# A state-space scan kernel: one three-bank feed tile with a single VectorE multiply, and work of the joins moved between engines

## The chip, the cores and the metric

One core of a Trainium2 chip runs the whole kernel. The metric is the device time of one execution in microseconds (us). The engines are named as in the profile: PE (TensorE), DVE (VectorE), ACT (ScalarE), POOL (GpSimd) and SP (SyncE, which only issues DMAs here).

## The reference

Eight images of 64 x 64 x 96 go through two layers. Nearly all the work is the selective scan of the first: for each image four directions, 192 channels and 16 states, over 4096 positions.

```python
xc = silu(conv3x3_depthwise(x @ in_proj_w.T [first half]) + conv_b)
xs = stack([s0, s1, s0[..., ::-1], s1[..., ::-1]])      # diagonal, antidiagonal, both reversed
dts, Bs, Cs = split(xs @ x_proj_weight)
delta = softplus(dts @ dt_projs_weight + dt_projs_bias)
def step(hst, inp):
    u_t, d_t, B_t, C_t = inp
    hst = hst * exp(d_t[..., None] * A) + (d_t * u_t)[..., None] * B_t[:, :, None, :]
    return (hst, einsum('bkdn,bkn->bkd', hst, C_t))
y = ys + Dk * xs, summed over the four directions, back in image order
yn = (y - mean) * rsqrt(var + 1e-5) * ln_w + ln_b
out = yn * silu(z) @ out_proj_w.T
```

Then come a residual sum, attention without softmax, and a feed-forward layer with fp8 products.

## The kernel before

**Steps and iterations.** `run` cuts each image into 16 steps: `q` = 0 walks the positions forward in 8 chunks of 512, `q` = 1 backward. Two directions and 64 channels fill the 128 partitions, so the 192 channels are G = 3 groups. A step has 16 iterations, one for each state `n`; 2048 iterations in all form the main loop (L1169 to L1206). An iteration works on tiles of 128 x 3 x 512.

**One iteration.** ACT makes the decay, exp(delta A), by three activations, two iterations ahead (L985, three buffers). The feed, (delta u) times a row of B, is made in PSUM in one of three ways, which FEED (L48) names for each state:
- "A" (10 of 16): ACT scales the transposed product `duT` by B into `feedT`, eight activations (L1007), two iterations ahead; PE transposes it back into the feed (`turn`, L1015), four transposes for each group.
- "G" (1 of 16): the same with POOL's multiplies (L998).
- "D" (5 of 16: states 0, 2, 4, 8, 10): PE copies the row of B to all partitions of feed 0 by a product with `pick` (L1017), and DVE multiplies it by `du`, three instructions, the last of them in place (L1032).

DVE then runs three recurrences (`scan`, L1028), one for each group, `h = decay * h + feed`. POOL keeps the last column (L1042) and multiplies h by the row of C, `cc` (L1047), an iteration later. Four iterations behind, PE transposes h into `y`, three banks that gather the 16 states (`reduce`, L1061). After a step's last state `place` copies `y` to SBUF by ACT and stores it: for q = 0 into `part` (L1090), for q = 1 into the two images `wide` (L1104). For q = 1 the stored part is loaded at state 0 (L1056), into the tile of `place`, and added to `y` by three products with the identity (L1074).

**PSUM.** Its eight banks are `y` (three), two work banks, and three tiles `feed0` to `feed2` of one bank each (L896). Before the main loop, and after it, the feed tiles serve as work banks too; after it, so does a tile `y_end` of three banks, cut into three.

**The order on each engine** is the program's. `tc.manual_schedule()` leaves it as written, and waits between engines are derived from which instructions touch which tile. L1192 to L1197 write PE's order within an iteration: the feed transposes of one group for the next iteration, four y transposes, background work, and the same for the next group. DVE's background work stands between scan 1 and scan 2 (L1035).

**Background work** (convolution of the next image, `front`; normalisation, projection, attention and feed-forward of the last one, `tail`) is written as generators that yield an engine and an estimate in us before each piece. `Work.at` lets pieces go at fixed places of an iteration, within a credit for each engine (L274), and LAGS (L239) says how many iterations a piece stands behind the one that it needs.

**prologue** makes what a step needs, two steps ahead: B and C rows, delta by softplus, `du` by POOL (L947, two buffers), its transpose `duT` with three ACT copies (L955).

**join**, in `tail`, takes 512 positions: it sums the two images y by products with the identity (L665), which ACT copies out (L672) while DVE takes statistics from PSUM (L675); normalises by ACT (L681); transposes (L687); multiplies by the gate on DVE (L689); projects with weights into which ln_w and ln_b were folded (L701, L704); copies out (L708) and takes statistics again (L713). `layers` does the same at L809 and L813. The last image's tail runs after the main loop, with eight jobs at once and no scans beside it.

Of the kernel before, what the change touches and what calls it, by code (L numbers as in the profile page):

```python
# [9 lines left out]
F32 = mybir.dt.float32  # L10
# [7 lines left out]
P = 128  # L18
# [48 lines left out]
def weights(tc, const, dram, w):  # L67
# [28 lines left out]
    k.skip = tile("skip", [P, G, P])  # L96
    k.w_ln = tile("w_ln", [HC, 2, DM])
    k.b_ln = tile("b_ln", [HC, 2, DM])
    k.w1q = tile("w1q", [DM, HID], F8)
# [92 lines left out]
    def layers():  # L192
# [7 lines left out]
        yield SPIN  # L200
        with tc.tile_pool(name="prep", bufs=1, side="right") as prep:
            w_out = load("w_out", [HC, 2, DM], w["w_out"], pool=prep)
            ln_w = load("ln_w", [HC, 2], w["ln_w"], pool=prep)
            ln_b = load("ln_b", [HC, 2], w["ln_b"], pool=prep)
            for _ in range(2):
                yield SPIN

            for a in range(2):
                nc.vector.tensor_scalar(k.w_ln[:, a, :], w_out[:, a, :], ln_w[:, a : a + 1], None, ALU.mult)
                nc.vector.tensor_scalar(k.b_ln[:, a, :], w_out[:, a, :], ln_b[:, a : a + 1], None, ALU.mult)  # L210
        with tc.tile_pool(name="prep", bufs=1, side="right") as prep:
# [404 lines left out]
def tail(tc, work, x, out, k, at, b, last=False):  # L616
# [4 lines left out]
    with tc.tile_pool(name=f"t1_{b}", bufs=1, **area) as p1:  # L621
# [5 lines left out]
        with tc.tile_pool(name=f"t2_{b}", bufs=8 if last else 2, **area) as p2:  # L627
# [3 lines left out]
            def join(c):  # L631
# [22 lines left out]
                if last:  # L654
                    yield dve(2.5)
                    nc.vector.tensor_tensor(yn, ys[0], ys[1], ALU.add)
                    for i in range(4):
                        nc.vector.bn_stats(st[:, i, :], yn[:, i, :])
                        nc.vector.bn_aggr(mv[:, i, :], st[:, i, :])
                for j in range(0 if last else 2):  # L660
                    ps = yield bank(0.65)
                    v = view(ps, P, 2, DI)
                    for i in range(2):
                        for d in range(2):
                            nc.tensor.matmul(  # L665
                                v[:, i, :], k.ident, ys[d][:, 2 * j + i, :],
                                start=(d == 0), stop=(d == 1), skip_group_check=True,
                            )
                        if i == 0:
                            yield pe(0.65)  # L670
                    yield act(0.5)
                    nc.scalar.copy(yn[:, 2 * j : 2 * j + 2, :], v)  # L672
                    yield dve(1.0, 0)
                    for i in range(2):
                        nc.vector.bn_stats(st[:, 2 * j + i, :], v[:, i, :])  # L675
                        nc.vector.bn_aggr(mv[:, 2 * j + i, :], st[:, 2 * j + i, :])
                    work.release(ps)
                r, m = yield from rsqrt(nc, p2, k, mv, P, 4, "n")
# [4 lines left out]
                for a in range(2):  # L683
                    ps = yield bank(0.45)
                    v = view(ps, HC, CH)
                    for i in range(4):
                        nc.tensor.transpose(v[:, i * P : (i + 1) * P], yn[:, i, a * HC : (a + 1) * HC], k.ident)  # L687
                    yield dve(0.7)
                    nc.vector.tensor_tensor(yg[:, a, :], v, gate[:, a, :], ALU.mult)  # L689
                    work.release(ps)  # L690
                ps = yield bank(0.65)
                po = view(ps, P, 4, DM)
# [3 lines left out]
                for i in range(4):  # L696
                    if i % 2 == 0:
                        yield pe(1.2)
                    tok = slice(i * P, (i + 1) * P)
                    for a in range(2):  # L700
                        nc.tensor.matmul(  # L701
                            po[:, i, :], yg[:, a, tok], k.w_ln[:, a, :], start=False, stop=False, skip_group_check=True
                        )
                        nc.tensor.matmul(  # L704
                            po[:, i, :], gate[:, a, tok], k.b_ln[:, a, :], start=False, stop=(a == 1), skip_group_check=True
                        )
                yield act(0.5)
                nc.scalar.copy(t, po)  # L708
                if not last:
                    nc.sync.dma_start(out=at.mid[:, s, :], in_=t)  # L710
                yield dve(1.7, 0)
                for i in range(4):
                    nc.vector.bn_stats(st[:, i, :], po[:, i, :])  # L713
                    nc.vector.bn_aggr(mv[:, i, :], st[:, i, :])
                work.release(ps)
                r, m = yield from rsqrt(nc, p2, k, mv, P, 4, "a")
# [66 lines left out]
        with tc.tile_pool(name=f"t3_{b}", bufs=8 if last else 3, **area) as p2:  # L783

            def layers(c):
# [24 lines left out]
                st, mv = tile("st", [P, 4, 6]), tile("mv", [P, 4, 2])  # L810
                yield dve(1.7, 0)
                for i in range(4):
                    nc.vector.bn_stats(st[:, i, :], po[:, i, :])  # L813
                    nc.vector.bn_aggr(mv[:, i, :], st[:, i, :])
                work.release(ps)
                r, m = yield from rsqrt(nc, p2, k, mv, P, 4, "f")
# [43 lines left out]
def run(tc, psum, dram, x, out, w, NB):  # L860
# [34 lines left out]
    made, decays, feeds, hs, carry, sums, other = {}, {}, {}, {}, {}, {}, {}  # L895
    feed = [psum.tile([P, T], F32, tag=f"feed{g}", name=f"feed{g}") for g in range(G)]  # L896
    banks = [psum.tile([P, T], F32, tag=f"bank{i}", name=f"bank{i}") for i in range(2)]
    work = Work(banks + feed)

    def prologue(m):  # L900
# [44 lines left out]
        yield gp(3.4)  # L945
        du = o.du = tile("du", [P, G, T])
        nc.gpsimd.tensor_tensor(du, delta, u, ALU.mult)  # L947
# [11 lines left out]
    def bring(m):  # L959

        b, q, c = steps[m]
        work.finish(lambda: c in image(b).walked)
        u = pool.tile([P, G, T], F32, tag="u", name=f"u_{m}", bufs=2)
        made[m] = SimpleNamespace(u=u, c={})
        for d in range(2):
            nc.sync.dma_start(
                out=u[d * GC : (d + 1) * GC],
                in_=image(b).seq[d][:, c * T : (c + 1) * T].rearrange("(g i) t -> i g t", i=GC),
            )
# [49 lines left out]
    def recur(i):  # L1019
        m, n = divmod(i, NS)  # L1020
        _, q, _ = steps[m]
        h = hs[i] = pool.tile([P, G, T], F32, tag="h", name=f"h_{i}", bufs=6)
        a = decays.pop(i)
        back = slice(None, None, -1) if q else slice(None)

        def scan(g):
            init = carry[m - 1][:, n, g : g + 1] if m % NST else 0.0
            nc.vector.tensor_tensor_scan(h[:, g, back], a[:, g, back], feed[g][:, back], init, ALU.mult, ALU.add)  # L1028

        if FEED[n] == "D":  # L1030
            for g in (1, 2, 0):
                nc.vector.tensor_tensor(feed[g], feed[0], made[m].du[:, g, :], ALU.mult)  # L1032
        scan(0)
        scan(1)
        work.at("V")  # L1035
        scan(2)
# [12 lines left out]
    def reduce(i, part):  # L1049
        m, n = divmod(i, NS)  # L1050
        b, q, c = steps[m]
        if n == 0 and part == 0:
            sums[m] = psum.tile([P, TB * G, P], F32, tag="y", name=f"y_{m}")
            if q:
                other[m] = pool.tile([P, TB * 2 * DI], F32, tag="ys", name=f"y0_{m}")
                nc.sync.dma_start(out=other[m], in_=image(b).part[:, c, :])  # L1056
        y = sums[m]
# [7 lines left out]
        if q and n in (1, 2, 3) and part == 2:  # L1065
            for j in range(4 * (n - 1), 4 * n):
# [4 lines left out]
                )  # L1071
        if q and n in (8, 9, 10) and part == 2:
            j = n - 8
            nc.tensor.matmul(  # L1074
                y[:, 4 * j : 4 * j + 4, :].rearrange("p a c -> p (a c)"), w.ident,
                other[m][:, j * T : (j + 1) * T], start=False, stop=False, skip_group_check=True,
            )
        if part == 2:
            hs.pop(i)

    def place(m):
# [5 lines left out]
        ys = pool.tile([P, TB * 2 * DI], F32, tag="ys", name=f"ys_{m}")  # L1087
        if q == 0:
            nc.scalar.copy(ys, y.rearrange("p j c -> p (j c)"))
            nc.sync.dma_start(out=image(b).part[:, c, :], in_=ys)  # L1090
            return
        rows = ys.rearrange("p (d k c) -> p d k c", d=2, k=TB)
        for d in range(2):
            nc.scalar.copy(
                rows[:, d].rearrange("p k (g i) -> p k g i", i=GC),
                y.rearrange("p (k g) (d i) -> p d k g i", g=G, d=2)[:, d],
            )
            stride = (3 * WW + 1) * DI if d == 0 else (3 * WW - 1) * DI
            for v in range(2):
                for again in range(2):  # L1100
                    first = (c * (T // HH) + v + (again + d) * WW) * DI
                    view = image(b).wide[d][first : first + HH * stride].rearrange("(h x) -> h x", x=stride)
                    view = view[:, 0 : TB * 2 * DI].rearrange("h (k x) -> h k x", k=TB)[:, :, 0:DI]
                    nc.sync.dma_start(out=view, in_=rows[v * HH : (v + 1) * HH, d])  # L1104

    def begin(b):
# [62 lines left out]
    for i in range(total + LAG + 1):  # L1169
        m, n = divmod(i, NS)  # L1170
        b, at = divmod(i, PER)
        if i < total:
            if at == LAG + 1 and b:
                work.finish(all_done)
                work.stream(between(b))
# [28 lines left out]
        if i + 4 < total:  # L1204
            fetch(i + 4)
        feeds.pop(i, None)  # L1206

    work.finish(all_done)
# [83 lines left out]
```

## Time and profile before

| what | us |
|---|---|
| median of 3 runs | 11580.11 (11578.98 to 11580.71) |
| the profiled execution | 11584.24 |
| its span | 11582.5 |
| first scan begins | 243.8 |
| last scan ends | 11318.2 |
| granted TensorE clock, mean | 0.913 |

The main loop is 11,074 us of the span, 5.4 us an iteration. A step without background work takes 73 to 76 us, one beside the convolution 84 to 95, one beside joins 95 to 103, one beside the other layers 82 to 92.

In the profile, a group's line gives line, engine, operation, tile written and tiles read, shapes and count; then busy time in us and the mean of one in ns; then idle time just before them with what ended it. A timeline line gives start, duration, engine, line, operation, tiles and count, and in brackets the idle time before with what ended it.

### The profile page before, as it was taken

Reading aid. Unit: us, or ns where it says so; the run is one execution under the profiler, and the core shown is the slowest. Engines: PE = TensorE matmul, PEld = TensorE weight load, DVE = VectorE, ACT = ScalarE, POOL = GpSimd, SP = SyncE. Lnnn points to the kernel's source line nnn. Section 1 sums busy time; section 2 is a strip of 40 time slices with the busy share of each in tenths; the row PEclk is TensorE's granted clock in tenths of the full one; section 3 lists DMA queues with packets and bytes.
Section 4 is the critical chain, followed back from the end, with each engine's and each line's share of the span. In section 5 each row is a group of like instructions: output and inputs, shape, how many; then the busy total and the mean of one; then the engine's idle time right before and its main releaser. Section 6 shows DMA issues by size and latency. Waiting matters only on the chain.

```text
span 11582.5 us, 187413 instructions
## 1 busy us (share of the span) xinstructions
PE 9540.5 (82%) x63189; PEld 7973.6 (69%) x63189; DVE 9483.5 (82%) x10714; ACT 9430.0 (81%) x19571; POOL 8885.1 (77%) x6799
## 2 busy tenths in 40 slices
PE   6898889788888888888888888988889888887885
PEld 5677677676776667766677766767667676676663
DVE  2988888888878888788887888888888878888893
ACT  3888888878888888888888788887888878888883
POOL 1877887778867887777887788777887778878883
PEclk8999899898999989999899998999999889898996
DMA  3335333533335333353334433354333533332332
GB/s 91 105 91 140 100 91 91 144 107 97 98 96 134 108 105 91 106 135 104 97 98 113 125 100 104 92 133 116 100 92 98 131 107 96 100 97 86 99 97 53
DMA packets 1122757, 1207.26 MB, mean 104 GB/s; under 512 B 452789, under 2 KB 730006, under 8 KB 1121798
## 3 DMA queue, kind: packets, MB, share of 16 engines
q1 hardware_dynamic: 1121798, 1195.28, 37.6%
q8 instruction: 503, 8.24, 0.3%
q14 instruction: 456, 3.74, 0.1%
HBM read 874.83 MB, written 319.98 MB: 103 GB/s over the span
## 4 chain that ended last, share of the span: by engine, by line
PE 25%; POOL 21%; ACT 20%; DVE 15%; issue 11%; DMA 5%; SPq 3%; POOLq 0%; DVEq 0%; ACTq 0%
POOL h L1047 15%; DVE h L1028 9%; ACT feedT L1007 8%; PE y L1061 7%; PE feed L1015 6%; ACT decay L985 6%; DVE feed L1032 3%; DMA cc<-crow 3%; POOL du L947 2%; PE bank L550 2%; PE bank L915 2%; SPq L595 2%; POOL feedT L998 2%; PE bank L953 1%; POOL carry L1042 1%
## 5 line engine op out<-in xcount | busy, mean ns | idle before, releaser
L1047 POOL TENSOR_TENSOR h<-h,cc 128x1536 f32<-128x1536 f32 x2048 | 7076.9, 3455 | 368.8 <-DMA cc<-crow 187.1
L1028 DVE TENSOR_TENSOR_SCAN h<-decay,carry,feed 128x512 f32<-128x512 f32 x5376 | 6529.7, 1263 | 987.1 <-PE feed L1015 769.8
L985 ACT ACTIVATE decay<-delta,a_neg 128x512 f32<-128x512 f32 x6144 | 3971.1, 712 | 1156.1 <-DVE h L1028 1153.3
L1015 PE MATMUL feed<-ident,feedT 128*128 128x128 f32 x16896 | 3066.7, 301 | 1605.6 <-DVE h L1028 1070.5
L1061 PE MATMUL y<-ident,h 128*128 128x128 f32 x24576 | 3820.9, 288 | 127.2 <-POOL feedT L998 112.8
L1015 PEld LDWEIGHTS feed<-ident,feedT 128*128 128x128 f32 x16896 | 2178.8, 153 | 2288.1 <-ACT feedT L1007 882.8
L1007 ACT ACTIVATE feedT<-duT,rows 128x192 f32<-128x192 f32 x10240 | 3672.2, 444 | 23.8 <-PE feed L1015 21.2
L1061 PEld LDWEIGHTS y<-ident,h 128*128 128x128 f32 x24576 | 3127.9, 150 | 515.5 <-issue 335.2
L1042 POOL COPY carry<-h 128x3 f32<-128x3 f32 x2048 | 393.0, 192 | 1615.3 <-DVE h L1028 1545.8
L1032 DVE TENSOR_TENSOR feed<-feed,du 128x512 f32<-128x512 f32 x1920 | 1202.4, 687 | 137.2 <-PE feed L1017 134.6
L1028 DVE TENSOR_TENSOR_SCAN h<-decay,feed 128x512 f32<-128x512 f32 x768 | 882.5, 1201 | 127.3 <-PE feed L1015 87.5
L550 PE MATMUL bank<-wf,xp 97*128 97x192 f32 x4266 | 858.7, 332 | 0.0
L550 PEld LDWEIGHTS bank<-wf,xp 97*128 97x128 f32 x4266 | 691.0, 194 | 24.1 <-issue 13.5
L1017 PE MATMUL feed<-x,pick 77*128 77x512 f32 x1280 | 695.7, 626 | 3.4
L947 POOL TENSOR_TENSOR du<-delta,u 128x1536 f32<-128x1536 f32 x128 | 441.0, 3445 | 316.1 <-ACT delta L942 309.4
L915 PE MATMUL bank<-wx,u 128*128 128x77 f32 x3048 | 413.1, 299 | 36.2 <-DMA u<-seq 36.2
L915 PEld LDWEIGHTS bank<-wx,u 128*128 128x128 f32 x3048 | 407.3, 217 | 44.4 <-issue 39.6
L937 PE MATMUL bank<-x,ws 13*128 13x512 f32 x764 | 434.7, 649 | 1.6 <-ACT x L928 1.6
L998 POOL TENSOR_TENSOR feedT<-duT,rows 128x512 f32<-128x512 f32 x384 | 396.0, 1061 | 0.0
L955 ACT COPY duT<-bank 128x512 f32<-128x512 f32 x383 | 220.7, 576 | 176.4 <-PE bank L953 174.3
L939 DVE COPY delta<-bank 128x512 f32<-128x512 f32 x382 | 256.2, 671 | 56.4 <-PE bank L937 53.6
L1017 PEld LDWEIGHTS feed<-x,pick 77*128 77x128 f32 x1280 | 209.7, 197 | 71.7 <-DVE h L1028 39.5
(278 smaller groups left out, 7544.3 us busy)
## 6 DMA issues: line engine op xcount, KB each, us to landing
cc<-crow SPq DMA_DIRECT2D x4096, 128.0 KB
u<-seq SPq DMA_DIRECT2D x256, 384.0 KB
wide<-ys SPq DMA_DIRECT2D x512, 192.0 KB
ut<-image SPq DMA_DIRECT2D x768, 64.0 KB
seq<-us SPq DMA_DIRECT2D x128, 384.0 KB
part<-ys SPq DMA_DIRECT2D x64, 768.0 KB
y<-part SPq DMA_DIRECT2D x64, 768.0 KB
y<-wide SPq DMA_DIRECT2D x256, 192.0 KB
```

What stands on the lines that cost most here:

```text
L550: nc.tensor.matmul(v[:, j, :], flat[:, o : o + P], k.wf[:, i, :], start=(i == 0), stop=(i == 8), skip_group_check=True)
L915: nc.tensor.matmul(v[:, j, :], u[:, g, j * P : (j + 1) * P], w.wx[:, q, g, :], start=(g == 0), stop=(g == G - 1))
L947: nc.gpsimd.tensor_tensor(du, delta, u, ALU.mult)
L985: nc.scalar.activation(decays[i][:, g, :], made[m].delta[:, g, :], AF.Exp, scale=w.a_neg[:, q, g, n : n + 1])
L998: nc.gpsimd.tensor_tensor(f.rearrange("p (j g) (d c) -> p g j d c", g=G, d=d)[:, g], o.duT.rearrange("p (j g) (d c) -> p g j d c", g=G, d= ...
L1007: nc.scalar.activation(f[part], o.duT[part], AF.Copy, scale=o.rows[:, j, XB + d * NS + n : XB + d * NS + n + 1])
L1015: nc.tensor.transpose(feed[g][:, j * P : (j + 1) * P], feeds[i][:, j * G + g, :], w.ident)
L1017: nc.tensor.matmul(feed[0], w.pick[:, FEED[:n].count("D"), :], made[m].x, start=True, stop=True)
L1028: nc.vector.tensor_tensor_scan(h[:, g, back], a[:, g, back], feed[g][:, back], init, ALU.mult, ALU.add)
L1032: nc.vector.tensor_tensor(feed[g], feed[0], made[m].du[:, g, :], ALU.mult)
L1047: nc.gpsimd.tensor_tensor(hs[i], hs[i], c.unsqueeze(1).to_broadcast([P, G, T]), ALU.mult)
L1061: nc.tensor.matmul(y[:, j, :], hs[i][:, g, r * P : (r + 1) * P], w.ident, is_transpose=True, start=(n == 0 and j % 4 == 0), stop=(n == NS ...
```

## The change

It has these parts:
- The three feed tiles become one tile of three banks, and DVE's three multiplies become one instruction over it, with the groups in reverse order so that bank 0, which is read, is written last.
- `du` gets one buffer instead of two, and waits in the program's order until the step before has made its last "D" multiply (state 10).
- join sums the two y on POOL and takes statistics from SBUF. The gate's multiply leaves DVE: ACT applies ln_w and ln_b on the way out of PSUM, and POOL multiplies by the gate. The projection is one product for each half. Statistics at L713 and L813 read the copy in SBUF, and the bank is released before them.
- place copies by halves for q = 0 too. For q = 1 the part is loaded at state 8 into a tile of its own and added by POOL (`spread`), which then issues the stores.
- The streams of the next image start two iterations later.

```diff
-    feed = [psum.tile([P, T], F32, tag=f"feed{g}", name=f"feed{g}") for g in range(G)]
+    feeding = psum.tile([P, G, T], F32, tag="feed", name="feed")
+    feed = [feeding[:, g, :] for g in range(G)]
...
         yield gp(3.4)
-        du = o.du = tile("du", [P, G, T])
+        while m and not made[m - 1].multiplied:
+            yield "G", 0.0, -1, False
+        du = o.du = tile("du", [P, G, T], 1)
...
         if FEED[n] == "D":
-            for g in (1, 2, 0):
-                nc.vector.tensor_tensor(feed[g], feed[0], made[m].du[:, g, :], ALU.mult)
+            nc.vector.tensor_tensor(
+                feeding[:, ::-1, :], feed[0].unsqueeze(1).to_broadcast([P, G, T]), made[m].du[:, ::-1, :], ALU.mult
+            )
+        if n == FEED.rindex("D"):
+            made[m].multiplied = True
...
-            if q:
-                other[m] = pool.tile([P, TB * 2 * DI], F32, tag="ys", name=f"y0_{m}")
-                nc.sync.dma_start(out=other[m], in_=image(b).part[:, c, :])
+        if q and n == 8 and part == 0:
+            other[m] = pool.tile([P, TB * 2 * DI], F32, tag="y0", name=f"y0_{m}")
+            nc.sync.dma_start(out=other[m], in_=image(b).part[:, c, :])
...
-        if q and n in (8, 9, 10) and part == 2:
-            j = n - 8
-            nc.tensor.matmul(
-                y[:, 4 * j : 4 * j + 4, :].rearrange("p a c -> p (a c)"), w.ident,
-                other[m][:, j * T : (j + 1) * T], start=False, stop=False, skip_group_check=True,
-            )
...
+    def spread(m, rows):
+        b, q, c = steps[m]
+        for d in range(2):
+            yield gp(1.8, 1)
+            nc.gpsimd.tensor_tensor(
+                rows[:, d], rows[:, d], other[m].rearrange("p (d k c) -> p d k c", d=2, k=TB)[:, d], ALU.add
             )
...
-            if at == LAG + 1 and b:
+            if at == LAG + 3 and b:
+                work.finish(lambda: all_done() and not other)
```

In join, with the same at the statistics of `layers`:

```diff
-                for j in range(0 if last else 2):
-                    ps = yield bank(0.65)
...
-                    yield act(0.5)
-                    nc.scalar.copy(yn[:, 2 * j : 2 * j + 2, :], v)
-                    yield dve(1.0, 0)
...
+                else:
+                    yield gp(1.8)
+                    nc.gpsimd.tensor_tensor(yn, ys[0], ys[1], ALU.add)
+                    yield dve(2.1)
+                for i in range(4):
+                    nc.vector.bn_stats(st[:, i, :], yn[:, i, :])
+                    nc.vector.bn_aggr(mv[:, i, :], st[:, i, :])
...
-                    yield dve(0.7)
-                    nc.vector.tensor_tensor(yg[:, a, :], v, gate[:, a, :], ALU.mult)
+                    yield act(0.7)
+                    nc.scalar.activation(
+                        yg[:, a, :], v, AF.Identity, scale=k.ln_w[:, a : a + 1], bias=k.ln_b[:, a : a + 1]
+                    )
                     work.release(ps)
+                yield gp(2.3)
+                nc.gpsimd.tensor_tensor(yg, yg, gate, ALU.mult)
...
-                            po[:, i, :], yg[:, a, tok], k.w_ln[:, a, :], start=False, stop=False, skip_group_check=True
-                        )
-                        nc.tensor.matmul(
-                            po[:, i, :], gate[:, a, tok], k.b_ln[:, a, :], start=False, stop=(a == 1), skip_group_check=True
+                            po[:, i, :], yg[:, a, tok], k.w_out[:, a, :], start=False, stop=(a == 1), skip_group_check=True
...
-                yield dve(1.7, 0)
+                work.release(ps)
+                yield dve(1.7)
                 for i in range(4):
-                    nc.vector.bn_stats(st[:, i, :], po[:, i, :])
+                    nc.vector.bn_stats(st[:, i, :], t[:, i, :])
```

In `weights`, ln_w and ln_b are loaded as they are, and the two folded weights and their four DVE instructions go.

More of the change, by code (lines that the diff above doesn't have):

```diff
@@ L96, in weights @@
     k.skip = tile("skip", [P, G, P])
-    k.w_ln = tile("w_ln", [HC, 2, DM])
-    k.b_ln = tile("b_ln", [HC, 2, DM])
     k.w1q = tile("w1q", [DM, HID], F8)
@@ L200, in layers @@
         yield SPIN
[L201 to L210, printed above, removed]
+        k.w_out = load("w_out", [HC, 2, DM], w["w_out"])
+        k.ln_w = load("ln_w", [HC, 2], w["ln_w"])
+        k.ln_b = load("ln_b", [HC, 2], w["ln_b"])
+        yield SPIN
         with tc.tile_pool(name="prep", bufs=1, side="right") as prep:
@@ L656, in join @@
                     nc.vector.tensor_tensor(yn, ys[0], ys[1], ALU.add)
-                    for i in range(4):
-                        nc.vector.bn_stats(st[:, i, :], yn[:, i, :])
-                        nc.vector.bn_aggr(mv[:, i, :], st[:, i, :])
-                for j in range(0 if last else 2):
-                    ps = yield bank(0.65)
-                    v = view(ps, P, 2, DI)
-                    for i in range(2):
-                        for d in range(2):
-                            nc.tensor.matmul(
-                                v[:, i, :], k.ident, ys[d][:, 2 * j + i, :],
-                                start=(d == 0), stop=(d == 1), skip_group_check=True,
-                            )
-                        if i == 0:
-                            yield pe(0.65)
-                    yield act(0.5)
-                    nc.scalar.copy(yn[:, 2 * j : 2 * j + 2, :], v)
-                    yield dve(1.0, 0)
[L674 to L677, printed above, removed]
+                else:
[5 more added lines that the diff above has]
+                    nc.vector.bn_aggr(mv[:, i, :], st[:, i, :])
                 r, m = yield from rsqrt(nc, p2, k, mv, P, 4, "n")
@@ L697, in join @@
                     if i % 2 == 0:
-                        yield pe(1.2)
+                        yield pe(0.65)
                     tok = slice(i * P, (i + 1) * P)
@@ L710, in join @@
                     nc.sync.dma_start(out=at.mid[:, s, :], in_=t)
-                yield dve(1.7, 0)
+                work.release(ps)
+                yield dve(1.7)
                 for i in range(4):
-                    nc.vector.bn_stats(st[:, i, :], po[:, i, :])
+                    nc.vector.bn_stats(st[:, i, :], t[:, i, :])
                     nc.vector.bn_aggr(mv[:, i, :], st[:, i, :])
-                work.release(ps)
                 r, m = yield from rsqrt(nc, p2, k, mv, P, 4, "a")
@@ L810, in layers @@
                 st, mv = tile("st", [P, 4, 6]), tile("mv", [P, 4, 2])
-                yield dve(1.7, 0)
+                work.release(ps)
+                yield dve(1.7)
                 for i in range(4):
-                    nc.vector.bn_stats(st[:, i, :], po[:, i, :])
+                    nc.vector.bn_stats(st[:, i, :], t[:, i, :])
                     nc.vector.bn_aggr(mv[:, i, :], st[:, i, :])
-                work.release(ps)
                 r, m = yield from rsqrt(nc, p2, k, mv, P, 4, "f")
@@ L963, in bring @@
         u = pool.tile([P, G, T], F32, tag="u", name=f"u_{m}", bufs=2)
-        made[m] = SimpleNamespace(u=u, c={})
+        made[m] = SimpleNamespace(u=u, c={}, multiplied=False)
         for d in range(2):
@@ L1071, in reduce @@
                 )
-        if q and n in (8, 9, 10) and part == 2:
-            j = n - 8
-            nc.tensor.matmul(
-                y[:, 4 * j : 4 * j + 4, :].rearrange("p a c -> p (a c)"), w.ident,
-                other[m][:, j * T : (j + 1) * T], start=False, stop=False, skip_group_check=True,
-            )
         if part == 2:
@@ L1087, in place @@
         ys = pool.tile([P, TB * 2 * DI], F32, tag="ys", name=f"ys_{m}")
[L1088 to L1091, printed above, removed]
         rows = ys.rearrange("p (d k c) -> p d k c", d=2, k=TB)
@@ L1096, in place @@
                 y.rearrange("p (k g) (d i) -> p d k g i", g=G, d=2)[:, d],
+            )
+        if q == 0:
+            nc.sync.dma_start(out=image(b).part[:, c, :], in_=ys)
+        else:
+            work.start(spread(m, rows), urgent=True)
+    def spread(m, rows):
[4 more added lines that the diff above has]
+                rows[:, d], rows[:, d], other[m].rearrange("p (d k c) -> p d k c", d=2, k=TB)[:, d], ALU.add
             )
@@ L1104, in place @@
                     nc.sync.dma_start(out=view, in_=rows[v * HH : (v + 1) * HH, d])
+        other.pop(m)
     def begin(b):
@@ L1206, in run @@
         feeds.pop(i, None)
+    work.finish(lambda: not work.urgent)
     work.finish(all_done)
```

## The prediction, made before the result was known

> **What bounds the kernel now.** First the table of engines and the chain of work that ended last.
>
> ```profile
> PE 9540.5 (82%) x63189; PEld 7973.6 (69%) x63189; DVE 9483.5 (82%) x10714; ACT 9430.0 (81%) x19571; POOL 8885.1 (77%) x6799
> PE 25%; POOL 21%; ACT 20%; DVE 15%; issue 11%; DMA 5%; SPq 3%; POOLq 0%; DVEq 0%; ACTq 0%
> ```
>
> No engine is full and none owns the chain: the kernel lives on overlap. So the costliest groups are read next, for what the overlap is between.
>
> ```profile
> L1028 DVE TENSOR_TENSOR_SCAN h<-decay,carry,feed 128x512 f32<-128x512 f32 x5376 | 6529.7, 1263 | 987.1 <-PE feed L1015 769.8
> L1015 PE MATMUL feed<-ident,feedT 128*128 128x128 f32 x16896 | 3066.7, 301 | 1605.6 <-DVE h L1028 1070.5
> L1032 DVE TENSOR_TENSOR feed<-feed,du 128x512 f32<-128x512 f32 x1920 | 1202.4, 687 | 137.2 <-PE feed L1017 134.6
> ```
>
> The feed is a ring of two: PE writes it (L1015, L1017), DVE reads it (L1028), and each waits for the other, some 1 us at a time. Only 987 us of DVE's 11,582 go to this, because the three feeds are three tiles: once scan 0 is over, PE refills feed 0 while DVE runs scans 1 and 2. The timeline of PE, then of DVE, shows that:
>
> ```profile
> 3003.84 0.63 PE L1015 MATMUL feed<-ident,feedT 128*128 128x128 f32 x4 [2.12 <-DVE h L1028]
> 3004.86 0.66 PE L1015 MATMUL feed<-ident,feedT 128*128 128x128 f32 x4
> 3005.97 0.66 PE L1015 MATMUL feed<-ident,feedT 128*128 128x128 f32 x4
> ...
> 3002.47 6.78 DVE L1028 TENSOR_TENSOR_SCAN h<-decay,feed 128x512 f32<-128x512 f32 x6
> ```
>
> The three fours start 1.0 to 1.1 us apart, at the pace of the scans, and DVE runs six scans without a pause.
>
> The change makes the three tiles one tile of three banks. What happens then is in this trace, in its last 200 us: there the tile y_end (three banks, used as three work banks) stands beside the tiles feed, with the same instructions.
>
> ```profile
> 11392.46 5.27 PE L687 MATMUL feed<-ident,y 128*96 128x128 f32 x12
> 11394.26 0.69 DVE L689 TENSOR_TENSOR yg<-feed,gate 96x512 f32<-96x512 f32 x1 [1.07 <-PE feed L687]
> 11396.08 0.69 DVE L689 TENSOR_TENSOR yg<-feed,gate 96x512 f32<-96x512 f32 x1 [1.14 <-PE feed L687]
> 11397.72 5.26 PE L687 MATMUL y_end<-ident,y 128*96 128x128 f32 x12
> 11403.02 1.28 DVE L689 TENSOR_TENSOR yg<-y_end,gate 96x512 f32<-96x512 f32 x2 [4.57 <-PE y_end L687]
> ...
> 11424.78 0.48 ACT L708 COPY t<-feed 128x384 f32<-128x384 f32 x1 [3.74 <-PE feed L704]
> 11441.67 1.24 ACT L708 COPY t<-y_end 128x384 f32<-128x384 f32 x3 [12.18 <-PE y_end L704]
> ...
> 11537.67 0.56 ACT L836 CAST h<-y_end 128x512 f16<-128x512 f32 x1
> 11538.28 1.44 PE L834 MATMUL y_end<-xq,w1q 96*128 96x512 fp8e5 x3 [0.99 <-ACT h L836]
> ```
>
> From the tiles feed, a read starts after each four matmuls (1.8 us apart). From y_end the first read starts after all twelve, 4.57 us idle, though its own bank was full after four; ACT's three copies come together after 12.18 us. The other direction too: PE writes y_end again 0.05 us after the third read's end (11537.67 + 0.56), though the first bank's read began at 11535.19. So the program's waits treat a PSUM tile as a whole, whichever bank is touched. This decides the forecast.
>
> **The change part by part. The feed's tile** (L896). With one tile, refill waits for scan 2 instead of scan 0, and scan 0 waits for the last refill instead of the first. The loop then alternates: DVE alone, PE alone. Prices, all from this trace:
> - From a scan's end to PE's start 0.15 us (median of 826); from the last transpose's start to the scan's 0.41 us (739 cases).
> - Between them PE issues, in the order of L1192 to L1197, 12 feed transposes with the first 8 of the y transposes between: 19 steps of 0.11 us, 2.1 us. A gap of **2.65 us** ahead of an iteration fed by transposes, 11 of 16, 1408 in all.
> - Ahead of a "D" iteration only the pick is between: 0.15 us, and 1.06 from its start to the multiply's: **1.21 us**, 640 times.
> - Three scans back to back: 2 x 1.12 + 1.26 = 3.50 us, 2048 times.
> - Other DVE work that L1035 puts between scan 1 and scan 2 now delays PE: 777 us from first to last scan, L689 (which goes) left out. Other PE work lying between the feed transposes: 694 us, without the removed lines.
>
> **The multiply** (L1032). Three take 1.87 us from first start to last end. One of 1536 elements is not in the trace. Rows: 687 ns for 512, 958 for 768 (L656); the slope of 1.06 ns an element gives 958 + 768 x 1.06 = 1.77 us. Bounds 1.60 and 1.88. Taken: 1.77, 640 times, a gain of 64 us.
>
> Sum at full TensorE clock: 1408 x 2.65 = 3731; 640 x 1.21 = 774; 2048 x 3.50 = 7168; 640 x 1.77 = 1133; 777; 694; the stretch ahead of the first scan 244 and behind the last 264. Total **14,785 us**.
>
> **The clock.** PE now pauses in every iteration, some 2.5 to 3.5 us. After pauses with full pace before them, the trace shows half pace (0.21 us a step instead of 0.11) in 16 of 61 cases at 2 to 2.5 us, 14 of 26 at 2.5 to 3, and 65 of 101 at 3 to 3.5. One such case, which lasts 3.3 us:
>
> ```profile
> 3012.54 1.08 PE L1015 MATMUL feed<-ident,feedT 128*128 128x128 f32 x4 [3.01 <-ACT decay L985]
> ...
> 3015.90 0.60 PE L1015 MATMUL feed<-ident,feedT 128*128 128x128 f32 x4
> ```
>
> A slow gap: 0.15 + 15 steps at 0.215 + 5 at 0.11 + 0.41 = 4.35 us, 1.70 more; a slow pick 0.85 more. All slow would add 1408 x 1.70 + 640 x 0.85 = 2938 us: 17,723. I take 55%, near the middle row: 14,785 + 1616 = **16,401**.
>
> The Trainium skill ("TensorE: Matmul & The Clock Gate", Part 1: The HAM clock gate) has the half rate return only after a whole idle window of about 3.4 us; by that most gaps would stay fast and the sum would be near 14,800. The rows above show it after shorter pauses, and they are taken.
>
> **du** (L946). One buffer instead of two, so POOL's multiply moves from iteration 3 of a step to iteration 10, after the last "D", and the three copies L955 (0.576 us) from 5 to 7 to 12 to 14, where ACT has feedT and decay each time (2.86 + 1.95 us). DVE now idles 3.06 us at iteration 14, most of it for PE and ACT. With today's overlap two copies would land on that path, 128 x 2 x 0.576 = 147 us. In the forecast an iteration there takes 3.50 + 2.65 = 6.15 us or more, over ACT's 4.8, and covers them.
>
> **join.** L665's 896 matmuls (182 us) and L672's copies go; POOL adds: by its rows (384 elements 914 ns, 1536 elements 3455) 768 cost 1.76 us, 56 times, 99 us. The gate: DVE's L689 (78 us) becomes an ACT pass (a row like it, L515, 772 ns; 128 times, 99 us) and a POOL multiply of 1024 (2.33 us, 64 times, 149 us). L704's 1024 matmuls (203 us) go. The statistics read SBUF an iteration later, so DVE no longer waits for ACT there: L675 109.5, L713 135.8, L813 71.7 us today, some 280 us of it inside the loop. **place.** L1074 goes (197 us of PE), 128 POOL adds of 768 come (225 us); the 8 stores of a step wait for POOL rather than ACT, on an SP queue that waits 3,199 us for POOL already, ahead of fetches made four iterations early. POOL gets 473 us in all. In the forecast all this lies in the longer iterations: POOL would be busy 9,360 of 16,401 us. Uncovered it costs what the third rival says. The other load (L1056) comes 8 iterations later into its own tile, 8 ahead of its use; the weights' edits lie in the first 244 us; the split copy for q = 0 adds 64 x 0.15 = 10 us to ACT, under the same cover; the next image's streams start two iterations later.
>
> **The rivals.** *Full clock:* the same alternation, PE kept fast by its background work: 14,785. For it: the granted clock was 0.96 in the stretch 4346 to 4780. Against: those stretches have PE 89% busy; here it would be near 60%.
> *Bank by bank, faster:* waits follow the banks after all, and the overlap stays. Gains: 64 + 78 + 280 = 422 us of DVE; half is taken, as DVE idles there for PE too: 11,370, between 11,160 and 11,580. For it: the feedT tile in SBUF is followed part by part (L1015 waits for single copies). Against: y_end, three times. The Trainium skill ("PSUM — Partial Sum Buffer", The four PSUM rules) says that each bank is a separate memory; by that the banks need no common wait, and the sum would be this one. The y_end rows show the wait all the same.
> *Bank by bank, slower:* the same overlap, but POOL sets the pace where tail's joins run: it is 74 us busy in steps of 95 to 102 there, gets 10 of joins and 3.5 of place, and DVE's statistics now stand behind it; it decides once POOL runs more than an iteration (5.4 us) late, as it does by 8 us at iteration 3 today. With the 147 us of du: about 11,800.
>
> **How the numbers follow.** Alternation with a mixed clock 0.70, at full clock 0.18, bank by bank faster 0.07, slower 0.03, no change 0.02. 0.2% (23 us) is about what a measurement of this kernel can tell from no change. Predicted 16,401 us. Bounds: 14,785 and 17,723 with some 100 to 200 us for terms read off medians: 14,600 to 17,900. The profiled execution took 11,584.2 us with a span of 11,582.5, 4 us above the median of the runs, which is nothing here.
>
> **What would show it.** DVE idle ahead of the multiply and of scan 0 for PE in every iteration, 4,500 us or more in all; PE's L1015 idle for L1028 as large; no L1015 starting during scans 1 and 2; granted clock well below 0.91; DVE, ACT and POOL 55 to 65% busy; L1032's successor at 1.6 to 1.9 us; L713's wait for ACT gone. Wrong if feed transposes start while scans of the same iteration run: then the rival by banks holds.

## The result, and the profile after

The changed kernel takes 17,276 us, median of 4 runs (17,247 to 17,280), against 11,580 us for the kernel before: 1.492 times, 95% interval 1.489 to 1.495. The forecast was 16,401 us, with 14,600 to 17,900 as its range.

The table of engines and the granted clock of the profiled execution after (span 17,245.0 us):

```profile
PE 11490.0 (67%) x60885; PEld 9798.4 (57%) x60885; DVE 9330.8 (54%) x9302; ACT 9621.6 (56%) x19651; POOL 9405.3 (55%) x7047
...
PEclk7687778777787777877778777887778777777776
```

DVE, ACT and POOL did as much work as before, within 6%, in half as much time again. PE's busy time rose by 1,950 us though it has 2,304 matmuls fewer: its clock fell from 0.913 to 0.766. Time was lost in waits and in clock, not in work. The groups around the feed say between whom:

```profile
L1010 DVE TENSOR_TENSOR_SCAN h<-decay,carry,feed 128x512 f32<-128x512 f32 x5376 | 6561.0, 1264 | 5533.5 <-PE feed L997 4956.6
L997 PE MATMUL feed<-ident,feedT 128*128 128x128 f32 x16896 | 3647.3, 356 | 3804.6 <-DVE h L1010 3631.4
L1014 DVE TENSOR_TENSOR feed<-feed,du 128x1536 f32<-128x1536 f32 x640 | 1130.6, 1767 | 1113.0 <-PE feed L999 1113.0
```

The scans last as long as before (1,264 ns against 1,263), but DVE idles 5,533 us ahead of them instead of 987, and PE idles 3,805 us ahead of its feed transposes instead of 1,606. The one multiply takes 1,767 ns, and DVE waits ahead of each, 1.7 us on average.

The timeline of DVE, then of PE, in a step without background work (start, duration, engine, line, operation, count, idle before):

```profile
6619.30 3.44 DVE L1010 TENSOR_TENSOR_SCAN h<-decay,feed 128x512 f32<-128x512 f32 x3 [4.78 <-PE feed L997]
6627.06 3.44 DVE L1010 TENSOR_TENSOR_SCAN h<-decay,feed 128x512 f32<-128x512 f32 x3 [4.33 <-PE feed L997]
...
6622.89 0.67 PE L997 MATMUL feed<-ident,feedT 128*128 128x128 f32 x4 [2.87 <-DVE h L1010]
6623.35 1.06 PE L1047 MATMUL y<-ident,h 128*128 128x128 f32 x4
6624.20 1.06 PE L997 MATMUL feed<-ident,feedT 128*128 128x128 f32 x4
6625.06 1.06 PE L1047 MATMUL y<-ident,h 128*128 128x128 f32 x4
6625.91 1.02 PE L997 MATMUL feed<-ident,feedT 128*128 128x128 f32 x4
```

The scans end at 6622.74. Only then, 0.15 us later, does PE begin to refill feed 0, whose scan was over 2 us before. DVE starts again 1.15 us after the third four began, when all three banks are full. The two engines take turns, here and everywhere: of the 1,408 iterations fed by transposes, none has a feed transpose that begins before scan 2 of the iteration before has ended; in the kernel before, 1,316 have. The first four after the pause of 2.87 us take 0.67 us; the 1.06 us behind them, where the kernel before mostly shows 0.60, is PE at half pace.

Taken from the starts and ends of the whole trace, the same terms as in the forecast:

| term | forecast, us | measured, us |
|---|---|---|
| gap ahead of 1408 iterations fed by transposes, clock and PE background included | 5742 | 6203 |
| gap ahead of the multiplies, clock included | 1073 | 1096 |
| three scans with DVE's background between | 7945 | 8191 |
| multiply to scan 0 | 1133 | 1209 |
| before the first scan, after the last | 508 | 545 |
| sum (of the unrounded terms) | 16,401 | 17,245 |

### The profile page after: what moved, and what is told of

Its sections match the earlier page's. It is cut to its first block, busy times and chain, and to the rows that moved or that the text cites. A ratio compares the mean times of both kernels' runs of the same rounds, so it can differ in the third digit from the quotient of the medians.

```text
span 17245.0 us, 178820 instructions
## 1 busy us (share of the span) xinstructions
PE 11490.0 (67%) x60885; PEld 9798.4 (57%) x60885; DVE 9330.8 (54%) x9302; ACT 9621.6 (56%) x19651; POOL 9405.3 (55%) x7047
## 5 line engine op out<-in xcount | busy, mean ns | idle before, releaser
L1010 DVE TENSOR_TENSOR_SCAN h<-decay,carry,feed 128x512 f32<-128x512 f32 x5376 | 6561.0, 1264 | 5533.5 <-PE feed L997 4956.6
L997 PE MATMUL feed<-ident,feedT 128*128 128x128 f32 x16896 | 3647.3, 356 | 3804.6 <-DVE h L1010 3631.4
L997 PEld LDWEIGHTS feed<-ident,feedT 128*128 128x128 f32 x16896 | 2795.1, 188 | 4270.4 <-issue 2554.9
L1047 PE MATMUL y<-ident,h 128*128 128x128 f32 x24576 | 5022.5, 354 | 2.4 <-POOL h L1033 1.9
L1047 PEld LDWEIGHTS y<-ident,h 128*128 128x128 f32 x24576 | 4259.3, 191 | 567.3 <-issue 549.3
L999 PE MATMUL feed<-x,pick 77*128 77x512 f32 x1280 | 1032.5, 900 | 1691.4 <-DVE h L1010 1691.4
L1014 DVE TENSOR_TENSOR feed<-feed,du 128x1536 f32<-128x1536 f32 x640 | 1130.6, 1767 | 1113.0 <-PE feed L999 1113.0
L542 PE MATMUL bank<-wf,xp 97*128 97x192 f32 x4266 | 992.4, 372 | 0.0
L542 PEld LDWEIGHTS bank<-wf,xp 97*128 97x128 f32 x4266 | 824.4, 226 | 6.4 <-issue 6.4
L1070 ACT COPY ys<-y 128x768 f32<-128x768 f32 x256 | 192.0, 802 | 665.3 <-PE y L1047 467.7
L917 PE MATMUL bank<-x,ws 13*128 13x512 f32 x764 | 519.5, 764 | 0.8 <-ACT x L908 0.8
```

Of the source, the lines that this page charges most:

```text
L542: nc.tensor.matmul(v[:, j, :], flat[:, o : o + P], k.wf[:, i, :], start=(i == 0), stop=(i == 8), skip_group_check=True)
L917: nc.tensor.matmul(ps, w.ws[:, q, g, :], x[0 : 2 * NR + 1, :], start=True, stop=True)
L997: nc.tensor.transpose(feed[g][:, j * P : (j + 1) * P], feeds[i][:, j * G + g, :], w.ident)
L999: nc.tensor.matmul(feed[0], w.pick[:, FEED[:n].count("D"), :], made[m].x, start=True, stop=True)
L1014: nc.vector.tensor_tensor(feeding[:, ::-1, :], feed[0].unsqueeze(1).to_broadcast([P, G, T]), made[m].du[:, ::-1, :], ALU.mult)
L1047: nc.tensor.matmul(y[:, j, :], hs[i][:, g, r * P : (r + 1) * P], w.ident, is_transpose=True, start=(n == 0 and j % 4 == 0), stop=(n == NS ...
```

## Experiments

**The tile alone, undone and done.** The first puts the three feed tiles and three multiplies back into the changed kernel. The second makes the feed one tile in the kernel before, with its three multiplies as they are. The diff shows the tiles in the first; the second has these lines the other way round.

```diff
-    feeding = psum.tile([P, G, T], F32, tag="feed", name="feed")
-    feed = [feeding[:, g, :] for g in range(G)]
+    feed = [psum.tile([P, T], F32, tag=f"feed{g}", name=f"feed{g}") for g in range(G)]
```

> The changed kernel with the feed as three tiles of one bank again and with VectorE's three multiplies; all the rest of the change stays. Theory (the one tile makes DVE and PE take turns): the overlap is back, feed transposes start while scans run, and the time is that of the bank-by-bank rivals, 11,370 us, between 11,160 and 11,800. Rival (the moved work, POOL's 473 us or du's new place, makes a good part of the 5,700 us): it stays above 13,000 us.

> The kernel before with one edit: feed0 to feed2 become slices of one tile of three banks; three multiplies, everything else as before. Theory: this edit alone costs it all. Against the changed kernel it has 640 x 0.10 = 64 us of multiplies, 78 us of gate multiplies and up to 280 us of waits behind ACT more on DVE, all in line now: 17,276 + 422 = 17,700 us, between 17,200 and 18,000. Rival (one tile is harmless, as each bank is waited for by itself): 11,580 us, within 1%.

The first took 11,239 us, 0.971 of the kernel before (0.970 to 0.973); the second 17,991 us in one run. So the edit of a tile's declaration costs some 6,400 us by itself in the kernel before, and 6,000 us together with the one multiply in the changed kernel; all the rest of the change is a gain of 332 us. Scans and multiplies, first in the run with three tiles, then in the kernel before with one:

```profile
L1009 DVE TENSOR_TENSOR_SCAN h<-decay,carry,feed 128x512 f32<-128x512 f32 x5376 | 6515.2, 1262 | 805.1 <-PE feed L996 690.2
```

```profile
L1029 DVE TENSOR_TENSOR_SCAN h<-decay,carry,feed 128x512 f32<-128x512 f32 x5376 | 6568.6, 1264 | 5732.3 <-PE feed L1016 5227.8
L1033 DVE TENSOR_TENSOR feed<-feed,du 128x512 f32<-128x512 f32 x1920 | 1342.7, 699 | 1112.2 <-PE feed L1018 1068.3
```

The idle time ahead of the scans goes with the tile, 805 against 5,732 us. The second run's three multiplies also take 2.17 us together, from first start to last end, instead of 1.88 (busy time 1,343 against 1,202 us). Scan 0 then starts 2.30 us after the first multiply, against 1.89 us in the changed kernel: inside one tile the single multiply gains 0.41 us and not 0.10.

**What lies in the gap.** If the engines take turns, what PE does between its feed transposes is paid in full, and so is what DVE does between its scans. The first run issues the 12 feed transposes ahead of everything else; the second also moves DVE's background work behind scan 2.

```diff
         for part in range(3):
             if i + 1 < total:
                 turn(i + 1, part)
+        for part in range(3):
             if 0 <= i - LAG < total:
                 reduce(i - LAG, part)
...
         scan(1)
-        work.at("V")
         scan(2)
+        work.at("V")
```

> The changed kernel with PE's order within an iteration altered: all 12 feed transposes first, then the 12 y transposes and the background work. Theory: the gap ahead of a scan loses 8 y transposes and 0.53 us of background work. In the changed kernel's trace it is 4.41 us; with 11 steps at a mixed clock (2.0 us) it is 0.15 + 2.0 + 0.46 = 2.6 us, 1,408 times: 17,276 - 2,530 = 14,750 us, between 14,300 and 15,200. Rival (what DVE waits for is not PE's turn but feedT from ACT, or POOL): within 200 us of 17,276.

> As the run before, and DVE's background work stands behind scan 2 instead of between scan 1 and scan 2. Theory: it now falls into the gap in which DVE waits for PE anyway, so its 777 us and some 200 us of waits inside the three scans leave the line: about 13,900 us, between 13,600 and 14,300. Rival (DVE itself is full): no change against the run before, within 100 us.

They took 14,571 and 13,392 us, one run each; the second lies below its stated bounds. The idle time ahead of the scans, in the first:

```profile
L1010 DVE TENSOR_TENSOR_SCAN h<-decay,carry,feed 128x512 f32<-128x512 f32 x5376 | 6562.1, 1264 | 3023.0 <-PE feed L997 2755.1
```

It is 3,023 us instead of 5,533. The mean gap went from 4.41 to 2.41 us, 2,812 us over 1,408 gaps. The time fell by 2,705, as the three scans with DVE's background between them grew from 4.00 to 4.14 us. On the timeline of the second, all 12 feed transposes now come at once, and the y transposes after them (the window ends at nine of these):

```profile
5005.51 2.79 PE L997 MATMUL feed<-ident,feedT 128*128 128x128 f32 x12 [4.40 <-DVE h L1010]
5008.09 2.13 PE L1047 MATMUL y<-ident,h 128*128 128x128 f32 x9
```

The 12 take 2.79 us here, slow again after a pause of 4.40 us. From the first run to the second the three scans, first start to last end, fell from 4.14 to 3.60 us, 1,104 us of the 1,179, where some 977 were expected. The granted clock rose with each step, from 0.766 to 0.818 and 0.850. Reordering wins back two thirds of the loss, with one tile still.

**Two banks in one tile.** On the run with three tiles, feeds 1 and 2 share one.

```diff
-    feed = [psum.tile([P, T], F32, tag=f"feed{g}", name=f"feed{g}") for g in range(G)]
+    pair = psum.tile([P, 2, T], F32, tag="feed", name="feed")
+    feed = [psum.tile([P, T], F32, tag="feed0", name="feed0"), pair[:, 0, :], pair[:, 1, :]]
```

> The run with three feed tiles, with feed 1 and feed 2 in one tile of two banks and feed 0 in a tile of its own; three multiplies. Theory (a tile is waited for as a whole): feed 0 is refilled during scans 1 and 2 as before, feeds 1 and 2 only after scan 2, while scan 0 of the next iteration runs (1.12 us). After scan 2 PE needs 0.15 + 11 steps at a mixed clock (1.6 to 2.0) + 0.41, less the 1.12: 1.1 to 1.5 us, 1,408 times, part of it in place of the 900 us that DVE waits there now: 11,239 + 1,300 to 2,000, about 12,900 us, between 12,300 and 13,500. Rival (the loss comes from three banks together, or from bank 0 being shared with the pick): 11,240 us, within 1%.

12,224 us in one run, 985 more than with three tiles: the price came out below the stated bounds. The place is as expected. Feed 0 is refilled before the scan 2 ahead has ended in 1,362 of the 1,408 iterations (1,313 with three tiles), feed 1 in none (874 with three tiles). Summed by scan, DVE idles 1,704 us ahead of scan 1 (390 with three tiles) and 199 ahead of scan 0 (462). The timeline of DVE shows it:

```profile
4025.66 2.45 DVE L1010 TENSOR_TENSOR_SCAN h<-decay,carry,feed 128x512 f32<-128x512 f32 x2
4028.56 1.28 DVE L1010 TENSOR_TENSOR_SCAN h<-decay,carry,feed 128x512 f32<-128x512 f32 x1 [0.46 <-PE feed L997]
```

Scan 2 and the next scan 0 run without a pause; scan 1 waits for the shared tile.

**Where the 332 us come from.** Two of the rest's three parts alone on the kernel before, and the third, place, with du.

> The kernel before with the edits of the joins, the weights and the feed-forward layers' statistics alone (three feed tiles, three multiplies, du and place as before). The run with three tiles showed that the change without its one tile is 2.9% faster, 332 us. Theory: it is the joins that bring it, by DVE's waits behind ACT (280 us) and the gate's multiplies (78 us): about 11,290 us, between 11,210 and 11,400. Rival (du's new place brings it, as POOL's du and the feedT behind it hold 4% of the chain of before): 11,550 us, within 0.5%.

> The kernel before with du in one buffer and made after state 10, nothing else. Theory: two of duT's copies land where DVE waits for ACT, at most 147 us, and POOL's chain at states 3 to 6 gets shorter, 0.5 to 1 us a step, 64 to 128 us: about 11,600, between 11,500 and 11,720. Rival (du brings the gain): 11,350 us or less.

> The kernel before with du's new place and with the edits of place (the part added by POOL, loaded later into its own tile, streams two iterations later); place does not fit in SBUF without du's single buffer. Theory: as du alone, less part of PE's 197 us: about 11,560, between 11,450 and 11,700. Rival (POOL's 225 us more are on the path): 11,750 us or more.

They took 0.982 (0.981 to 0.984), 0.999 (0.998 to 1.000) and 0.995 (0.993 to 0.996) of the kernel before: 11,371, 11,563 and 11,516 us. The joins bring the most, 205 us, though less than the 285 expected; du's place brings 12 and place some 47 more. The parts add up to 264 of the 332; where the other 68 come from, and which of the joins' edits brings the 205, was not tried.

**One multiply without a shared tile.** On the run with three tiles, one instruction writes the products into h, in SBUF, and the scans of "D" iterations run over h in place.

```diff
-            nc.vector.tensor_tensor_scan(h[:, g, back], a[:, g, back], feed[g][:, back], init, ALU.mult, ALU.add)
+            nc.vector.tensor_tensor_scan(h[:, g, back], a[:, g, back], (h[:, g] if FEED[n] == "D" else feed[g])[:, back], init, ALU.mult, ALU.add)
...
-            for g in (1, 2, 0):
-                nc.vector.tensor_tensor(feed[g], feed[0], made[m].du[:, g, :], ALU.mult)
+            nc.vector.tensor_tensor(
+                h, feed[0].unsqueeze(1).to_broadcast([P, G, T]), made[m].du, ALU.mult
+            )
```

> The run with three feed tiles, with one multiply of 1536 elements all the same: it writes its product into the tile h in SBUF, and the scans run over h in place, so no PSUM tile spans banks. Theory: 640 x 0.10 = 64 us less DVE work on a path that is mostly DVE's in the D iterations, and feed 1 and 2 stand free for PE through a D iteration: 11,170 us, between 11,080 and 11,240. Rival (a scan with three inputs in SBUF is slower, or POOL and DVE get in each other's way there): 11,240 us or more.

12,636 us, 1.092 of the kernel before (1.090 to 1.094): a miss, and the rival's side. Its groups of scans, fed from PSUM and from SBUF, then DVE and POOL on the timeline:

```profile
L1009 DVE TENSOR_TENSOR_SCAN h<-decay,carry,feed 128x512 f32<-128x512 f32 x3696 | 4485.6, 1257 | 512.7 <-PE feed L996 475.1 <-POOL carry L1026 8.5 <-ACT decay L966 8.4
L1009 DVE TENSOR_TENSOR_SCAN h<-decay,carry,h 128x512 f32<-128x512 f32 x1680 | 3659.1, 2217 | 51.7 <-ACT feedT L988 0.9 <-DVE h L1012 0.9
```

```profile
5002.27 7.62 DVE L1009 TENSOR_TENSOR_SCAN h<-decay,carry,h 128x512 f32<-128x512 f32 x2
...
5001.04 3.47 POOL L1031 TENSOR_TENSOR h<-h,cc 128x1536 f32<-128x1536 f32 x1 [0.27 <-PE bank L549]
5004.45 4.36 POOL L928 TENSOR_TENSOR du<-delta,u 128x1536 f32<-128x1536 f32 x1
```

The scan over h takes 2,217 ns on average instead of 1,257. The two shown end at 5005.59 and 5009.89, 1.08 us behind the ends of POOL's two instructions (5004.51 and 5008.81), and POOL's du took 4.36 us instead of 3.45: one waits while the other runs. The last section counts such cases.

## Why the forecast held, point by point

The span after is 844 us longer than the sum forecast. The table's five terms are all too small, by 461, 23, 246, 76 and 37 us, so no error hides another between them.

**The whole-tile wait** was right: y_end's rows said what a three-bank tile would do, and the run with three tiles, the run with one tile in the kernel before, and the run with two banks shared each show it: PE waits for the last scan of the tile, and DVE for the tile's last transpose. The rule that each PSUM bank is a memory of its own (the Trainium skill, "PSUM — Partial Sum Buffer", The four PSUM rules) is not contradicted; it did not decide, because the program's waits are coarser than the banks.

**The fixed prices** were right: 0.15 us from a scan to PE and 0.41 from the last transpose to a scan (medians after: 0.146 and 0.409), and the multiply at 1.767 us against 1.77.

**The clock** was mis-sized: "I take 55%, near the middle row". The rows were counted in a kernel whose PE was 82% busy. After, PE's own time between the first and the last feed transpose, background taken out, is 3.27 us on average, against 2.09 at full pace. That is 1.18 of the 1.70 us between fast and slow, or 69%. It makes 345 us of the 461 missing in the first term. The rest is background between the transposes, 743 us instead of 694, and the two ends of the gap, 0.61 us together on average where the medians make 0.56. The price of a slow gap has a slip in it: it counts 20 steps (15 slow, 5 fast), the fast gap 19. With 19 a slow gap costs 1.58 us more and not 1.70, and the measured share is 75%; the slip hid 97 us of the error. That PE would stay fast by its background work (the rival of 14,785 us) fell.

The rows were sorted by the length of the pause; the trace shows more of the rule. In the trace after, the granted clock is recorded in stretches of 3.41 us, and the next one goes by how busy PE was in the one before. Full speed was lost after all 992 stretches with PE busy for less than 40%, and kept after all 281 with 90% or more; half speed ended after none of 512 with less than 70%, and after 1,175 of 1,375 with 90% or more. In the timeline above PE was busy for 16% of the stretch from 6619.93 us, and ran at half speed from 6623.35 to 6626.76.

**The scans** cost 246 us more than "2 x 1.12 + 1.26" with DVE's background added; the run with that work behind scan 2 shows the triple at 3.60 us without it, not 3.50, which makes 205 of the 246. The 1.12 us between starts was read off scans without a carry, as in the line at 3002.47; these are 768 of 6,144. With a carry three scans take 3.62 us back to back, without one 3.44 (both after).

**The smaller terms.** From the multiply to scan 0 the forecast took the multiply's own 1.77 us; scan 0 starts 0.12 us after its end, which makes the 76 us. Of the 37 us at the ends 32 lie before the first scan, which begins at 275.7 us instead of 243.8; with three tiles it begins at 247.8, so most of this goes with the tile too.

**The rest of the change.** What it adds to POOL and ACT was hidden under the alternation, as forecast: POOL is 55% busy, and the scans wait for POOL's multiplies by cc for 106 us in all. What it takes off DVE and PE was in line: the kernel before with one tile took 715 us more than the changed kernel (one run), 260 of them by its three multiplies. DVE's waits behind ACT at the statistics are down from 317 to 61 us. Without the alternation the rest is a gain too: the bank-by-bank rival had taken half of 422 us, 64 of them for the single multiply, and the run with three tiles, which has three multiplies, kept 332. Its slower twin, POOL as the bound, fell: there DVE waited 114 us for POOL's sums, a price well below what the joins bring. du's copies did not cost their 147 us.

## What to carry to other kernels

Look at what a wait covers before merging tiles to save instructions: 640 multiplies at 0.11 us saved, 72 us, were bought with 6,000 us of overlap. The kernel's own trace can hold the answer in a corner off the main loop, here in its last 200 us. And where two engines do take turns, order each one's work so that what the other waits for comes first: that alone was worth 2,705 us, and 1,179 more on the other engine.

## What was not expected of the hardware

In the run with the multiply into h, a DVE scan whose two data inputs both lie in SBUF did not run beside POOL's multiplies. Of these scans, 718 began while a multiply of POOL of over 3 us had 0.3 us or more left; nine in ten ended 1.077 to 1.085 us after that multiply, however much of it was left. The 435 such scans with next to no POOL instruction beside them (under 5% of their time) took 1.26 us on average; others reached 4.5. POOL paid too: the 95th percentile of its multiplies by cc was 4.35 us, the median 3.46. Scans with one input in PSUM took 1.25 us beside POOL (2,399 of them with POOL busy for 95% of their time or more). The Trainium skill ("SBUF — State Buffer", Who interferes with whom) tells of an exclusive lock on a port pair that VectorE and GpSimd share; the times here agree with it.
